# A deformable-convolution network on one core: the offset convolution's last two terms in halves of four rows

## The chip, the cores and the metric

The kernel runs on one core of a Trainium2 chip. The metric is the device time of one execution in microseconds; the kernel before takes 6531.28 us (median of 3 runs, 6528.49 to 6531.62).

A core has five engines that run side by side and wait for each other through semaphores: TensorE (matmuls and transposes, written PE; its weight loads PEld), VectorE (DVE), ScalarE (ACT), GpSimd (POOL) and SyncE (SP). GpSimd and SyncE mostly issue DMAs here. TensorE writes to PSUM only, from which ScalarE or VectorE copy.

## The reference

The input is x of shape 4 x 256 x 64 x 64 in 32-bit floats. A channel normalisation is followed by three modulated deformable 3 x 3 convolutions, then by a mixture of eight experts with two chosen per token. What matters here is one deformable layer:

```python
om = lax.conv_general_dilated(x, w_off, (1, 1), padding=...) + b_off[None, :, None, None]
off = om[:, :2 * K].reshape(B, K, 2, H, W)
mask = jax.nn.sigmoid(om[:, 2 * K:])
ys = gy + base_y + off[:, :, 0]
xs = gx + base_x + off[:, :, 1]
sampled = _bilinear(x, ys, xs) * mask[:, None]
out = jnp.einsum('bikhw,oik->bohw', sampled, w.reshape(O, C, K)) + b
```

K is 9. The first line is the offset convolution: an ordinary 3 x 3 convolution of 256 channels to 27. Its result says for every pixel and tap where to sample, and with what weight.

## The kernel before

An image is worked in 8 blocks of 512 pixels, 8 rows of 64 columns each. With 3 layers and 4 images that makes 96 blocks. Two things are done to each.

**The offset convolution** (`off_block`, L345 and following). It has 18 terms: nine taps (ky, kx), each with two halves c of the channels. A term is one matmul with 128 rows of contraction, 27 (padded to 32) output channels and up to 512 pixels. As 32 outputs use a quarter of TensorE's columns, term m is put into column strip g = m % 4 and adds into its own 32 partitions of the PSUM tile po. Terms with kx = 1 come first and cover all 64 columns of a row (512 pixels); those with kx = 0 or 2 lack one column at the image's edge (8 x 63 = 504 pixels). So strips 0 and 1 get five terms, strips 2 and 3 four. A 32-bit matmul appears as two records in the trace, two passes over the same data, each with a weight load. `om` (L366) takes po out of PSUM on ScalarE with the bias; four matmuls `pm` (L371) add the strips and turn the result, so that pixels lie on partitions; then ScalarE and VectorE work out indices idx and coefficients cf.

**The main block** (`main_block`). For each of 9 taps and 4 groups of 128 pixels, GpSimd gathers the pixels' neighbours from a table in DRAM (`g`, L503, 9 buffers), VectorE interpolates in two operations (L509, L514, the result `s`, 8 buffers), ScalarE scales s by the mask (L517), TensorE transposes (`tp`, L532, 3 PSUM buffers), ScalarE copies to sT (L535), and TensorE multiplies with the layer's weights into acc (L549).

Beside these two, the experts of images that are through are worked in small pieces (ftp L843, ph L859, py L877), the normalisation of the next images is done (tp_pre), and the rows finished are written back as tables.

The program is written as a weave: generators give a few steps each between two taps. From this, a scheduler of the build sets the final order of each engine's instructions by its own estimate of times. Each engine then works in that order, and an instruction that waits holds those behind it. So the matmuls of one offset convolution are often split into runs with other matmuls between.

Of the kernel before, what the change touches and what calls it, by code (L numbers as in the profile page):

```python
# [17 lines left out]
CC = C // P  # L18
# [5 lines left out]
RPB = BLK // W  # L24
# [5 lines left out]
Q = 32  # L30
NQ = P // Q
# [86 lines left out]
class Weave:  # L118
# [226 lines left out]
    def off_block(self, l, b, n, w):  # L345

        nc = self.nc
        nm = f"{l}_{b}_{n}"


        po = self.ps1.tile([P, BLK], F32, tag="po", name=f"po_{nm}")

        terms = [(ky, kx, c) for kx in (1, 0, 2) for ky in range(3) for c in range(CC)]
        for m, (ky, kx, c) in enumerate(terms):
            g = m % NQ
            x0, x1 = max(0, 1 - kx), min(W, W + 1 - kx)
            nc.tensor.matmul(  # L357
                po[g * Q : (g + 1) * Q, :].rearrange("q (r w) -> q r w", w=W)[:, :, x0:x1],
                lhsT=self.wo[l][:, 3 * ky + kx, c, :],
                rhs=w[:, c, ky : ky + RPB, x0 + kx - 1 : x1 + kx - 1],  # L360
                start=(m < NQ),
                stop=(m + NQ >= len(terms)),
                tile_position=(0, g * Q),
            )
        om = self.small.tile([P, BLK], F32, tag="om", name=f"om_{nm}")
        nc.scalar.activation(om, po, AF.Identity, bias=self.bo[l])  # L366
        yield
        pm = self.ps.tile([P, TPB, 3 * K], F32, tag="tp", name=f"pm_{nm}")
        for t in range(TPB):

            nc.tensor.matmul(  # L371
                pm[:, t, :],
                lhsT=om[:, t * P : (t + 1) * P],
                rhs=self.strips[:, : 3 * K],
                start=True,
                stop=True,
            )

        def small(tag, shape=(P, J, 2), dt=F32):
            return self.small.tile(list(shape), dt, tag=tag, name=f"{tag}_{nm}")  # L380

        idx = self.plan.tile([P, J], I32, tag=f"idx{b % 2}", name=f"idx_{nm}")
        cf = self.plan.tile([P, J, 3], F32, tag=f"cf{b % 2}", name=f"cf_{nm}")
        self.plans[l, b, n] = (idx, cf)

        th = small("th", (P, J))
        nc.scalar.activation(
            th.rearrange("p (t k) -> p t k", k=K), pm[:, :, 2 * K :], AF.Tanh, scale=0.5
        )
        pos = small("pos")  # L390
        nc.scalar.copy(pos.rearrange("p (t k) d -> p t (k d)", k=K), pm[:, :, : 2 * K])
        yield
        yield
        with self.after(self.last):
            nc.vector.tensor_tensor(
                pos, pos, self.base[:, n].rearrange("p t k d -> p (t k) d"), ALU.add
            )

        nc.vector.tensor_scalar(pos, pos, -1.0, float(H), ALU.max, ALU.min)
        pi = small("pi", dt=I32)  # L400
        nc.vector.tensor_copy(pi, pos)
        pf = small("pf")
        nc.vector.tensor_copy(pf, pi)
        yield
        up = small("up")
        nc.vector.tensor_tensor(up, pf, pos, ALU.is_gt)
        fl = small("fl")
        nc.vector.tensor_tensor(fl, pf, up, ALU.subtract)

        nfr = small("nfr")  # L410
        nc.vector.tensor_tensor(nfr, fl, pos, ALU.subtract)
        ixf = small("ixf", (P, J))
        nc.vector.scalar_tensor_tensor(
            ixf, fl[:, :, 0], float(TC), fl[:, :, 1], ALU.mult, ALU.add
        )
        nc.vector.tensor_scalar(idx, ixf, float(TC + 1), None, ALU.add)
        yield


        first = small("first")  # L420
        nc.vector.tensor_scalar(first, nfr, 1.0, LEAST, ALU.add, ALU.max)
        inv = small("inv")
        nc.vector.reciprocal(inv, first)
        corner = small("corner", (P, J))
        nc.vector.tensor_tensor(corner, first[:, :, 0], first[:, :, 1], ALU.mult)
        nc.vector.scalar_tensor_tensor(cf[:, :, 0:2], nfr, -1.0, inv, ALU.mult, ALU.mult)
        nc.vector.scalar_tensor_tensor(cf[:, :, 2], th, 1.0, corner, ALU.add, ALU.mult)
# [720 lines left out]
```

## Time and profile before

| | us |
|---|---|
| median of 3 runs | 6531.28 |
| profiled execution | 7434.65 |
| its span, first to last instruction | 7432.9 |
| mean granted TensorE clock, as a share | 0.932 |
| transposes tp (L532), busy | 1227.0 |
| acc (L549), busy | 3442.6 |
| experts ph and py (L859, L877), busy | 683.7 and 658.8 |
| gathers g (L503) on GpSimd, busy | 3650.6 |
| interpolation (L509, L514) on VectorE, busy | 2556.5 and 1656.7 |

The profile is of one execution with the recorder on, which takes longer than a plain run. A group's line gives its busy time, the mean of one instruction in ns, and the idle time of the engine just before it with what ended most of that. A line of waits gives who waited for whom: us in total, number of times, the longest. A line of the timeline gives start and length in us, then engine, line, operation, tiles and shapes, and how many instructions it merges. In the lines of slices each digit is the busy share, or the granted clock, of one fortieth of the span in tenths.

### The profile page before, as it was taken

What the parts mean: (1) busy time and instruction counts of PE and PEld (TensorE: products, weight loads), DVE (VectorE), ACT (ScalarE), POOL (GpSimd) and SP (SyncE); (2) the same over time, 40 slices, a digit from 0 to 9 for tenths busy, and PEclk for the clock granted to TensorE, in tenths of its full rate; (3) what the DMA queues carried; (4) which work ended last, traced back from release to release, by engine and by line L of the source; (5) the groups of instructions that cost most, each with busy time, mean ns of one, the idle gap of its engine ahead of it and who ended that gap; (6) DMA issues with size and microseconds to landing.
All of it is one profiled execution on the core that took longest, in us unless ns stands there. A gap on an engine that the chain in (4) does not pass through costs nothing. (4 is left out here: it accounts for less than half of the span.)

```text
span 7432.9 us, 88104 instructions
## 1 busy us (share of the span) xinstructions
PE 6352.4 (85%) x26500; PEld 3653.7 (49%) x26500; DVE 4932.4 (66%) x11467; ACT 3278.3 (44%) x7139; POOL 4441.2 (60%) x4245
## 2 busy tenths in 40 slices
PE   7888888888888898988877898898887889977887
PEld 3434443444445555555444454454554456644665
DVE  7767776888756666776855676666787554667521
ACT  3444444554444444554443444444453334444322
POOL 4555665666656665555666665665667664666543
PEclk8999999989999999999989999999998899988988
DMA  8889999999879888888888998888998876887644
GB/s 286 312 297 339 346 339 346 362 345 340 321 267 322 311 315 315 310 314 296 282 295 306 327 331 299 318 324 314 325 342 307 281 273 233 286 301 271 229 138 124
DMA packets 805210, 2228.40 MB, mean 300 GB/s; under 512 B 105016, under 2 KB 307768, under 8 KB 798976
## 3 DMA queue, kind: packets, MB, share of 16 engines
q0 software_dynamic: 551200, 1947.35, 73.0%
q1 hardware_dynamic: 253536, 275.41, 11.0%
q8 instruction: 214, 3.51, 0.2%
q14 instruction: 260, 2.13, 0.1%
HBM read 2165.40 MB, written 196.40 MB: 318 GB/s over the span
## 5 line engine op out<-in xcount | busy, mean ns | idle before, releaser
L503 POOL DMA_INDIRECT g<-tab,idx x3456 | 3650.6, 1056 | 2310.7 <-DVE s L514 975.8
L549 PE MATMUL acc<-sT,wk 128*128 128x512 f32 x6912 | 3442.6, 620 | 44.6 <-ACT r L580 17.0
L509 DVE SCALAR_TENSOR_TENSOR g<-g,cf 128x512 f32<-128x512 f32 x3456 | 2556.5, 743 | 274.2 <-DMA g<-tab,idx 249.9
L514 DVE SCALAR_TENSOR_TENSOR s<-g,cf 128x256 f32<-128x256 f32 x3456 | 1656.7, 482 | 1287.5 <-PE tp L532 561.4
L535 ACT COPY sT<-tp 128x512 f32<-128x512 f32 x1728 | 1010.7, 586 | 2052.0 <-PE tp L532 1137.3
L532 PE MATMUL tp<-ident,s 128*128 128x128 f32 x6912 | 1227.0, 287 | 635.7 <-ACT s L517 373.8
L517 ACT ACTIVATE s<-s,cf 128x256 f32<-128x256 f32 x3456 | 1630.8, 508 | 260.7 <-DVE s L514 157.0
L549 PEld LDWEIGHTS acc<-sT,wk 128*128 128x128 f32 x6912 | 1238.3, 200 | 916.2 <-issue 871.5
L532 PEld LDWEIGHTS tp<-ident,s 128*128 128x128 f32 x6912 | 880.9, 147 | 1607.0 <-issue 839.5
L859 PE MATMUL ph<-fzT,w 128*128 128x256 f32 x2608 | 683.7, 401 | 111.1 <-ACT hT L869 74.2
L877 PE MATMUL py<-w,hT 128*128 128x256 f32 x2608 | 658.8, 392 | 39.9 <-ACT hT L869 23.2
L859 PEld LDWEIGHTS ph<-fzT,w 128*128 128x128 f32 x2608 | 498.1, 200 | 256.2 <-ACT hT L869 92.7
L869 ACT ACTIVATE hT<-ph,w 128x256 f32<-128x256 f32 x652 | 279.2, 471 | 695.2 <-PE ph L859 388.3
L877 PEld LDWEIGHTS py<-w,hT 128*128 128x128 f32 x2608 | 486.6, 194 | 180.6 <-issue 69.4
L815 POOL DMA_INDIRECT zt<-z,tok x326 | 330.9, 1015 | 174.2 <-issue 90.3
L803 POOL DMA_INDIRECT w<-in_W,wrow x163 | 175.7, 1078 | 379.3 <-ACT sT L535 134.1
L357 PE MATMUL po<-win,wo 128*32 128x504 f32 (+1 forms) x2304 | 364.1, 613 | 11.2 <-issue 8.3
L918 POOL DMA_INDIRECT gy<-ys,slots x256 | 260.2, 1017 | 106.7 <-issue 79.7
L895 DVE TENSOR_TENSOR y<-py,w 128x512 f32<-128x512 f32 x163 | 111.8, 686 | 316.3 <-PE py L877 242.7
L366 ACT ACTIVATE om<-po,bo 128x512 f32<-128x512 f32 x96 | 66.0, 688 | 365.4 <-PE po L357 228.5
L357 PE MATMUL po<-win_pre,wo 128*32 128x504 f32 (+1 forms) x1152 | 191.2, 628 | 4.1 <-ACT om L366 3.3
L357 PEld LDWEIGHTS po<-win,wo 128*32 128x32 f32 x2304 | 74.4, 111 | 223.8 <-issue 190.5
(154 smaller groups left out, 3029.2 us busy)
## 6 DMA issues: line engine op xcount, KB each, us to landing
tab<-hv SPq DMA_DIRECT2D x512, 128.0 KB
g<-tab,idx POOLq DMA_INDIRECT x3456
ys<-y SPq DMA_DIRECT2D x163, 256.0 KB
tab<-h_pre SPq DMA_DIRECT2D x128, 256.0 KB
wk<-in_conv_w SPq DMA_DIRECT2D x117, 256.0 KB
xc_pre<-in_x SPq DMA_DIRECT2D x32, 512.0 KB
xr_tok<-in_x SPq DMA_DIRECT2D x32, 512.0 KB
t<-t_tok SPq DMA_DIRECT2D x32, 512.0 KB
```

What stands on the lines that cost most here:

```text
L357: nc.tensor.matmul(po[g * Q : (g + 1) * Q, :].rearrange("q (r w) -> q r w", w=W)[:, :, x0:x1], lhsT=self.wo[l][:, 3 * ky + kx, c, :], rhs= ...
L503: self.gathered = nc.gpsimd.indirect_dma_start(out=g.rearrange("p x s f -> p (x s f)"), out_offset=None, in_=self.table(*self.stages[i][:2 ...
L509: nc.vector.scalar_tensor_tensor(g[:, :, 0, :], g[:, :, 1, :], cf[:, j, 0:1], g[:, :, 0, :], ALU.mult, ALU.add,)
L514: self.last = nc.vector.scalar_tensor_tensor(s, g[:, 1, 0, :], cf[:, j, 1:2], g[:, 0, 0, :], ALU.mult, ALU.add)
L517: nc.scalar.activation(s, s, AF.Copy, scale=cf[:, j, 2:3])
L532: self.turned = nc.tensor.transpose(tp[:, c, u * P : (u + 1) * P], ss[u][:, c * P : (c + 1) * P], self.ident)
L535: nc.scalar.copy(self.sT[:, :, t0 * P : (t0 + 2) * P], tp)
L549: nc.tensor.matmul(self.acc[:, o, :], lhsT=self.wk[k][:, c, o * P : (o + 1) * P], rhs=sT[:, c, :], start=(k == 0 and c == 0), stop=(k == K ...
L815: self.nc.gpsimd.indirect_dma_start(out=zt, out_offset=None, in_=grp.zd, in_offset=bass.IndirectOffsetOnAxis(ap=grp.tok[:, j : j + 1], axi ...
L859: nc.tensor.matmul(ph[:, h, :], lhsT=w1[:, o : o + P], rhs=zT[:, c, :], start=(c == 0), stop=(c == CC - 1),)
L869: nc.scalar.activation(ht[:, h, :], ph[:, h, :], AF.Gelu, bias=w1[:, k : k + 1])
L877: nc.tensor.matmul(py[:, u, :], lhsT=hT[h // 2][:, h % 2, u * P : (u + 1) * P], rhs=w2[:, h * C : (h + 1) * C], start=(h == 0), stop=(h == ...
```

## The change

The 18 terms modulo four strips leave two over. These two (kx = 2, ky = 2, both channel halves) are split by rows: each becomes two matmuls over four rows (4 x 63 = 252 pixels), so that 20 matmuls are dealt over the four strips: four full ones and one half in each. The sum of the strips, which pm forms, is the same.

```diff
-        terms = [(ky, kx, c) for kx in (1, 0, 2) for ky in range(3) for c in range(CC)]
-        for m, (ky, kx, c) in enumerate(terms):
+        terms = [
+            (ky, kx, c, 0, RPB) for kx in (1, 0, 2) for ky in range(3) for c in range(CC)
+        ]
+        left = len(terms) % NQ
+        share = RPB * left // NQ
+        terms[-left:] = [
+            (*term[:3], r0, r0 + share)
+            for term in terms[-left:] for r0 in range(0, RPB, share)
+        ]
+        for m, (ky, kx, c, r0, r1) in enumerate(terms):
             g = m % NQ
             x0, x1 = max(0, 1 - kx), min(W, W + 1 - kx)
             nc.tensor.matmul(
-                po[g * Q : (g + 1) * Q, :].rearrange("q (r w) -> q r w", w=W)[:, :, x0:x1],
+                po[g * Q : (g + 1) * Q, :].rearrange("q (r w) -> q r w", w=W)[:, r0:r1, x0:x1],
                 lhsT=self.wo[l][:, 3 * ky + kx, c, :],
-                rhs=w[:, c, ky : ky + RPB, x0 + kx - 1 : x1 + kx - 1],
+                rhs=w[:, c, r0 + ky : r1 + ky, x0 + kx - 1 : x1 + kx - 1],
                 start=(m < NQ),
                 stop=(m + NQ >= len(terms)),
                 tile_position=(0, g * Q),
```

NQ is 4, RPB 8 (rows of a block), so left is 2 and share is 4. The first four matmuls, which start a strip's sum, stay whole.

## The prediction

> **What bounds the kernel now.** I read the page first (busy shares, slices, groups), then the waits engine by engine, then one offset convolution in the timeline.
>
> ```profile
> PE 6352.4 (85%) x26500; PEld 3653.7 (49%) x26500; DVE 4932.4 (66%) x11467; ACT 3278.3 (44%) x7139; POOL 4441.2 (60%) x4245
> PE   7888888888888898988877898898887889977887
> PEclk8999999989999999999989999999998899988988
> DMA  8889999999879888888888998888998876887644
> L357 PE MATMUL po<-win,wo 128*32 128x504 f32 (+1 forms) x2304 | 364.1, 613 | 11.2 <-issue 8.3
> L357 PE MATMUL po<-win_pre,wo 128*32 128x504 f32 (+1 forms) x1152 | 191.2, 628 | 4.1 <-ACT om L366 3.3
> ```
>
> TensorE is at 80 to 90% in every slice, and DMA nearly as high: two resources are close together. The offset convolution (L357) is 555 us of TensorE's 6352, in 3456 records: 96 blocks x 18 matmuls x 2 passes each.
>
> The profiled execution took 7434.65 us, the median run 6531.28; the recording costs 903 us. TensorE's 6352 us of recorded work is 97% of the shorter time, so I expect TensorE to be fuller in a plain run than the page shows. Whether DMA is slowed by the recording the page doesn't say. I count savings as absolute microseconds of TensorE work and take the same number off the median.
>
> ```profile
> PE tp L532 <- ACT s L517: 373.8, 174, 15.9
> POOL g L503 <- DVE s L514: 975.8, 457, 15.4
> DVE s L514 <- PE tp L532: 561.4, 349, 9.7
> DVE g L509 <- DMA g<-tab,idx: 249.9, 98, 10.3
> ACT om L366 <- PE po L357: 228.5, 72, 6.3
> ```
>
> (us in total, times, longest.) Read from the third line: VectorE stands 561 us because transposes haven't freed an s buffer; because VectorE stands, GpSimd waits 976 us for a free gather buffer. That is back pressure from TensorE. Against it stand 250 us in which VectorE waits for a gather's data, which a faster TensorE doesn't shorten. 561 of 811 us, 0.69, is my share of the kernel in which TensorE time is kernel time.
>
> ```profile
> 2027.34 0.16 PEld L357 LDWEIGHTS po<-win,wo 128*32 128x32 f32 x8 [0.76 <-ACT hT L869]
> 2027.34 3.59 PE L357 MATMUL po<-win,wo 128*32 128x512 f32 x28
> 2027.80 0.12 PEld L357 LDWEIGHTS po<-win,wo 128*32 128x32 f32 x4 [0.30 <-issue]
> 2028.23 0.12 PEld L357 LDWEIGHTS po<-win,wo 128*32 128x32 f32 x4 [0.31 <-issue]
> 2028.65 0.12 PEld L357 LDWEIGHTS po<-win,wo 128*32 128x32 f32 x4 [0.31 <-issue]
> 2029.07 0.12 PEld L357 LDWEIGHTS po<-win,wo 128*32 128x32 f32 x4 [0.31 <-issue]
> 2029.49 0.12 PEld L357 LDWEIGHTS po<-win,wo 128*32 128x32 f32 x2 [0.31 <-issue]
> 2029.92 0.12 PEld L357 LDWEIGHTS po<-win,wo 128*32 128x32 f32 x2 [0.31 <-issue]
> 2030.86 0.33 PE L532 MATMUL tp<-ident,s 128*128 128x128 f32 x1
> ```
>
> This is a block's last 14 matmuls, 28 passes. The loads come every 0.42 us in fours, one round ahead of their matmuls: four strips stream together, and a round lasts one stream. The last two loads are x2: terms 16 and 17 sit on strips 0 and 1 only, and two rounds (first and second pass) run with half the array empty. From 2027.34 to 2030.86 are 3.52 us: 8 rounds of 0.424 us plus 0.13 us of emptying the array.
>
> **What the Trainium skill says.** "TensorEngine Tiling (Array Packing)", Key Properties: tiles work independently, and changing the tiling mode drains TensorE. The trace agrees: fours start together, and leaving costs the 0.13 us above. "TensorE: Matmul & The Clock Gate", Part 3: packed matmuls start about 4 ns apart; within a round the records here are some 7 ns apart. The tiling page's Instruction Overhead gives a floor of about 60 cycles for a small free size; 252 columns are far above it. No run shows a 252-column strip matmul yet.
>
> **The change part by part.**
>
> 1. Removed: two rounds of 504 columns per block. Added: two rounds of 252 columns with four strips filled. Each of the four half matmuls has a load and a stream per pass: 2 matmuls, 4 loads and 4 streams more per block. For a round's length there are two bounds. Linear in columns: 0.424 x 252/504 = 0.212 us; the 128-column transposes (four in 0.43 us) against the 512-column acc (four in 1.72 us) support linearity. Load-bound: a strip's load lasts 0.106 to 0.110 us, four of them 7 ns apart, so a round can't be under about 0.13; if the second pass's loads came late I allow 0.30 at most. I take 0.212. Saved: 2 x 0.212 = 0.424 us per block, 96 blocks: 40.7 us. Rounds in stretches of lower clock (mean granted 0.932) are longer and save more. Bounds: at 0.30, 24 us; at 0.212 and the mean clock, 44 us.
>
> 2. Start stagger: the last round has four starts instead of two, 14 ns later for the last one: 96 x 0.014 = 1.3 us lost.
>
> 3. The order. The two kernels' instruction orders, laid side by side, show the same work on every engine apart from these matmuls. GpSimd's queue is unchanged; on SP a single input load (xc_pre_7) moves by four places during start-up, and that costs nothing next to gathers already queued. A block is split into runs, with other matmuls between: before in 252 runs over 96 blocks (42 times as 1, 3, 14 matmuls), after in 246 (39 times as 1, 3, 16; 4, 16 goes from 24 to 32 times). A run of one matmul at 2053.56 lets the next transposes start only at 2054.53: 0.97 us for a single matmul. Joining one costs nothing elsewhere, since a run of four takes the same two rounds. Six runs fewer: about 5 us, put between 0 and 6.
>
> 4. No new wait: the halves read the same window and write the same po, which one om (L366) reads. In front of that om ScalarE stands idle 228 us with the s activations queued behind it, so po's earlier end helps there too; I count it inside part 1.
>
> 5. Moved by the scheduler on ScalarE: about 150 times a copy sT (L535) moves ahead of an s activation (L517), 15 times the reverse. Such a copy waits for its transposes, then takes 0.586 us, and the s behind it waits. Nothing if s was early. TensorE waited for an s before 174 of some 1728 transposes groups, one in ten: 15 of the 150 would hurt, by 0.59 us each, 9 us; bound above by 150 x 0.59 = 88 us. I take nothing in the sum, because the 15 reverse moves and TensorE's earlier end push the other way, and put it in the range.
>
> Sum on TensorE: 40.7 - 1.3 + 5 = 44.4, say 45 us. Times 0.69: 31 us. 7434.65 becomes about 7404 under the recorder, and 6531.28 becomes 6500.
>
> **Rivals.**
>
> - Absorbed: DMA sets the pace (8 or 9 tenths busy; 249.9 us of VectorE waiting for gathers). TensorE then waits longer for s. A conversion of 0.1 to 0.5: 5 to 22 us saved, 6509 to 6526. Against it: the 976 us in which GpSimd can't even issue a gather.
> - More: full conversion plus ScalarE released earlier at om, and rounds at lower clock: 48 to 65 us, 6466 to 6483. For it: TensorE's 97% of the plain time.
> - It doesn't do what it says: halves don't overlap, or a half round costs as much as a full one. Then part 1 is zero and only the run count remains: 6526 to 6533. Against: every four consecutive strip matmuls overlap in the trace, also when a run starts on another strip.
> - Slower: part 5 decides. The sT copies ahead of s delay the transposes, then VectorE and the gathers. It costs 0.59 us plus the wait for the copy's own transposes, say 0.8 us each time it is exposed. It cancels my 31 us from about 40 exposed cases in 150, where the trace suggests 15; at 60 to 100 cases it costs 48 to 80 us, so the time is 6548 to 6580.
>
> **How the numbers follow.** Forecast 0.53 (6490 to 6508), more 0.08, absorbed 0.20, doesn't do what it says 0.05, slower 0.14. A measurement of this kernel tells about 0.2% (13 us) from no change. Faster by more than that: forecast, more, and 0.08 of absorbed, 0.69. Within: the other 0.12 of absorbed and the 0.05: 0.17. Slower 0.14. Range: 6472 to 6540 takes the forecast, the absorbed case, no effect and most of "more"; about 0.17 is left out, nearly all on the slow side. The 24 us bound of part 1 with conversion gives about 6511, inside.
>
> **What would show it.** Each block's last loads come as x4 and x4 instead of x2 and x2, 0.21 us apart, and the run of 16 ends about 3.1 us after its start instead of 3.52. L357's records become 3840, its busy time falls from 555 to about 515 us. If TensorE's busy time falls by 45 us while "tp waits for s" grows by as much, the absorbed case holds. If the wait of tp for s grows by more, with sT waiting in front of s on ScalarE, the slower case holds. Wrong outright: half rounds spaced 0.42 us.

## The result and the profile after

The changed kernel takes 6500.16 us (median of 5 runs, 6491.25 to 6506.63) against 6530.9 us (6528.49 to 6531.62): a ratio of 0.9951, 95% interval 0.9937 to 0.9966, a gain of some 31 us.

The chips of this study fall into two levels. On most, the kernel before takes about 6530 us; on one it takes about 7500 us. The profile that the prediction read, with its span of 7432.9 us and a granted TensorE clock of 0.932, belongs to the upper level, though the times beside it are of the lower one, where the clock is 0.976. A new profile of the unchanged kernel (run a0 below, span 6536.8 us) is therefore the one to hold against the profile after. Three lines of its page, the busy times and the two groups of the offset convolution:

```profile
PE 6070.7 (93%) x26500; PEld 3541.3 (54%) x26500; DVE 4957.5 (76%) x11467; ACT 3335.7 (51%) x7139; POOL 4432.4 (68%) x4245
L357 PE MATMUL po<-win,wo 128*32 128x504 f32 (+1 forms) x2304 | 338.5, 593 | 1.1 <-ACT win L580 0.6
L357 PE MATMUL po<-win_pre,wo 128*32 128x504 f32 (+1 forms) x1152 | 187.0, 618 | 4.1 <-ACT om L366 3.3
```

The same of the changed kernel, whose lines after L352 are numbered eight higher:

```profile
span 6498.1 us, 88881 instructions
PE 6025.0 (93%) x26884; PEld 3542.5 (55%) x26884; DVE 4960.6 (76%) x11467; ACT 3330.6 (51%) x7139; POOL 4424.2 (68%) x4245
L365 PE MATMUL po<-win,wo 128*32 128x504 f32 (+2 forms) x2560 | 306.8, 551 | 1.2 <-ACT win L588 0.6
L365 PE MATMUL po<-win_pre,wo 128*32 128x504 f32 (+2 forms) x1280 | 173.9, 577 | 4.2 <-ACT om L374 3.5
```

The offset convolution has 384 records more and 44.8 us less (525.5 to 480.7). TensorE as a whole loses 45.7 us, so nothing else on it grew. (Such totals move from one execution to the next: a second profile of the changed kernel, run f1 below, has 6037.2 us at a clock of 0.973 where this one has 6025.0 at 0.976. The offset convolution alone agrees to 1.5 us, 480.7 and 479.2.) The span loses 38.7 us between these two executions, and the medians 31 us.

The mechanism is seen in one block's last 16 matmuls in the timeline of the changed kernel (start us, length, then what):

```profile
2089.51 3.17 PE L365 MATMUL po<-win,wo 128*32 128x512 f32 x32
2091.66 0.12 PEld L365 LDWEIGHTS po<-win,wo 128*32 128x32 f32 x4 [0.31 <-issue]
2092.09 0.12 PEld L365 LDWEIGHTS po<-win,wo 128*32 128x32 f32 x4 [0.31 <-issue]
2092.61 0.44 PE L540 MATMUL tp<-ident,s 128*128 128x128 f32 x2
```

The loads now come in fours to the end. They run one round ahead of their matmuls: the load at 2092.09 stands at the start of the first half round and carries the weights of the second. The start times of the last two rounds' matmuls show the half rounds directly. In the profile before they start 0.43 us apart, in that of the changed kernel 0.22 us (granted clock 1.00 in both stretches):

```profile
2029.91 0.59 PE L357 MATMUL po<-win,wo 128*32 128x504 f32 x2
2030.34 0.59 PE L357 MATMUL po<-win,wo 128*32 128x504 f32 x2
```

```profile
2092.08 0.38 PE L365 MATMUL po<-win,wo 128*32 128x252 f32 x4
2092.30 0.38 PE L365 MATMUL po<-win,wo 128*32 128x252 f32 x4
```

From the last load to the next transposes are 0.52 us, two half rounds and the emptying of the array. In the kernel before the same stretch, from 2029.92 to 2030.86, is 0.94 us, two full rounds and the emptying. From the run's start to the next transposes are 3.10 us, where before it was 3.52.

Who waits, in the profile of a0 and then in that of the changed kernel (us in total, times, longest):

```profile
DVE g L509 <- DMA g<-tab,idx: 471.8, 408, 10.3
DVE s L514 <- PE tp L532: 200.0, 197, 5.0
PE tp L532 <- ACT s L517: 202.5, 235, 4.1
ACT om L366 <- PE po L357: 230.5, 88, 5.1
```

```profile
DVE g L517 <- DMA g<-tab,idx: 470.7, 429, 10.9
DVE s L522 <- PE tp L540: 163.2, 163, 4.9
PE tp L540 <- ACT s L525: 200.1, 233, 5.1
ACT om L374 <- PE po L365: 199.0, 88, 4.8
```

VectorE's wait for TensorE falls by 37 us and ScalarE's wait for po by 31 us; the wait for gathers stays. TensorE's wait for s stays as it was (202.5 and 200.1 us), so the scheduler's moves on ScalarE cost nothing that can be seen.

**Where the 31 us came from.** The two executions can be cut at the same copies sT (the 181st, 541st, 1261st and 1601st of 1728). The windows view then shows, for each stretch, its length, the busy time of the engines, the clock, the DMA share and GB/s. First a0, then the changed kernel:

```profile
0.00:665.00 665.00, 599.87 (x2818) 295.82 (x2818) 551.48 (x1458) 342.46 (x758) 401.01 (x413) 0.97 0.96 354
665.00:1791.00 1126.00, 1028.47 (x4355) 537.02 (x4356) 992.72 (x2405) 620.65 (x1311) 771.22 (x728) 0.96 0.99 380
1791.00:4288.00 2497.00, 2408.72 (x10562) 1394.68 (x10561) 1954.45 (x4269) 1339.41 (x2907) 1796.75 (x1699) 0.99 0.96 360
4288.00:5593.00 1305.00, 1224.82 (x5269) 744.09 (x5268) 961.08 (x2120) 672.78 (x1414) 900.88 (x867) 0.99 0.91 334
```

```profile
0.00:664.00 664.00, 592.43 (x2917) 296.58 (x2918) 552.71 (x1459) 343.20 (x758) 400.19 (x413) 0.97 0.96 355
664.00:1785.00 1121.00, 1022.29 (x4434) 536.24 (x4433) 992.11 (x2405) 620.02 (x1311) 774.66 (x728) 0.96 0.99 381
1785.00:4249.00 2464.00, 2382.60 (x10720) 1394.03 (x10719) 1955.48 (x4266) 1335.64 (x2905) 1782.91 (x1699) 0.99 0.97 365
4249.00:5551.00 1302.00, 1217.15 (x5317) 744.50 (x5316) 962.73 (x2121) 671.62 (x1413) 899.99 (x866) 0.99 0.91 335
```

In the first two stretches, with 44 of the 96 blocks, TensorE loses 14 us of work and the time falls by 6. In the third, with 40 blocks, it loses 26 us and the time falls by 33. In the second the DMA engines are busy 0.99 of the time; in the third TensorE is busy 96%. These are single executions, and a stretch is good to some 7 us (run e1 below, with the TensorE work of before, has 2490 us in the third). What the cuts suggested was two regimes, and experiments with the change in parts of the blocks.

### The profile page after: what moved, and what is told of

It is laid out like the page before. It is cut to its first block, busy times and chain, and to the rows that moved or that the text cites. A ratio compares the mean times of both kernels' runs of the same rounds, so it can differ in the third digit from the quotient of the medians.

```text
span 6498.1 us, 88881 instructions
## 1 busy us (share of the span) xinstructions
PE 6025.0 (93%) x26884; PEld 3542.5 (55%) x26884; DVE 4960.6 (76%) x11467; ACT 3330.6 (51%) x7139; POOL 4424.2 (68%) x4245
## 5 line engine op out<-in xcount | busy, mean ns | idle before, releaser
L557 PE MATMUL acc<-sT,wk 128*128 128x512 f32 x6912 | 3317.4, 601 | 13.5 <-ACT win L588 9.2
L525 ACT ACTIVATE s<-s,cf 128x256 f32<-128x256 f32 x3456 | 1669.2, 509 | 688.8 <-DVE s L522 638.2
L557 PEld LDWEIGHTS acc<-sT,wk 128*128 128x128 f32 x6912 | 1193.0, 193 | 833.0 <-issue 800.1
L540 PE MATMUL tp<-ident,s 128*128 128x128 f32 x6912 | 1199.7, 280 | 204.6 <-ACT s L525 200.1
L867 PE MATMUL ph<-fzT,w 128*128 128x256 f32 x2608 | 651.2, 386 | 37.6 <-DMA w<-in_W,wrow 19.4
L867 PEld LDWEIGHTS ph<-fzT,w 128*128 128x128 f32 x2608 | 478.3, 192 | 164.2 <-ACT hT L877 36.4
L365 PE MATMUL po<-win,wo 128*32 128x504 f32 (+2 forms) x2560 | 306.8, 551 | 1.2 <-ACT win L588 0.6
L941 DVE SCALAR_TENSOR_TENSOR ta<-gy,cw,ta 128x256 f32<-128x256 f32 x256 | 120.3, 478 | 100.0 <-DMA gy<-ys,slots 53.5
L365 PE MATMUL po<-win_pre,wo 128*32 128x504 f32 (+2 forms) x1280 | 173.9, 577 | 4.2 <-ACT om L374 3.5
```

What stands on the lines that cost most here:

```text
L365: nc.tensor.matmul(po[g * Q : (g + 1) * Q, :].rearrange("q (r w) -> q r w", w=W)[:, r0:r1, x0:x1], lhsT=self.wo[l][:, 3 * ky + kx, c, :], ...
L525: nc.scalar.activation(s, s, AF.Copy, scale=cf[:, j, 2:3])
L540: self.turned = nc.tensor.transpose(tp[:, c, u * P : (u + 1) * P], ss[u][:, c * P : (c + 1) * P], self.ident)
L557: nc.tensor.matmul(self.acc[:, o, :], lhsT=self.wk[k][:, c, o * P : (o + 1) * P], rhs=sT[:, c, :], start=(k == 0 and c == 0), stop=(k == K ...
L867: nc.tensor.matmul(ph[:, h, :], lhsT=w1[:, o : o + P], rhs=zT[:, c, :], start=(c == 0), stop=(c == CC - 1),)
```

## The experiments

Each run stands beside the kernel before on the same chip. "Theory A" is the prediction's even share of 0.69, "B" a share set by the gathers, "C" that the scheduler's order decides, "A2" that a saving counts in the stretches where TensorE is full and not in the others; A2 was formed after the first four runs.

**a0_before_again**: no edit.

> The kernel before, unchanged, with a new profile. The profile that the prediction was made from had a span of 7432.9 us, while the changed kernel's profile has 6498.1 us, near its plain time. If that first profile was a disturbed execution (and not a cost of recording), this one has a span near 6530 us. Theory A (0.69 of TensorE's time is kernel time): VectorE's waits for tp stay above its waits for gathers. Theory B (the gathers' DMA sets the pace): in a span of 6530 us VectorE waits longer for gathers than for tp, as in the changed kernel (470.7 against 163.2 us).

Ratio 1.0000 (0.9992 to 1.0008), span 6536.8 us. The first profile's extra time is no cost of recording. The waits are those of theory B: 471.8 us for gathers, 200.0 for transposes. TensorE's busy time is 6070.7 us where the first profile had 6352.4. Times the granted clocks, 0.976 and 0.932, both are some 5920 us: the same work at a lower clock (an estimate from these four numbers).

**e1_halves_two_strips**: the 20 matmuls of the change, on two strips.

```diff
-            for term in terms[-left:] for r0 in range(0, RPB, share)
+            for r0 in range(0, RPB, share) for term in terms[-left:]
...
-            g = m % NQ
+            g = m % NQ if m < 16 else (m - 16) % 2
...
-                stop=(m + NQ >= len(terms)),
+                stop=(m >= 14 and m not in (16, 17)),
```

> The same 20 matmuls with halves of four rows, but all four halves on strips 0 and 1, two after each other on each. TensorE's rounds are as long as before, and the instruction order is nearly that of before (27 of 16074 other TensorE instructions moved). Theory A: the gain is the two half-empty rounds alone, so this stands at the time before, 6531 us within 10 us. If splitting itself costs (more loads, more starts), it is slower by up to 0.03 us a block, 3 us. Rival: if halves were cheaper for another reason than the use of four strips, it would be near 6500 us.

6529.57 against 6533.23 us, ratio 0.9995 (0.9987 to 1.0004). The offset convolution takes 524.5 us of TensorE, in a0 525.5. Splitting alone neither costs nor gains; the four strips are what gains.

**e2_one_strip**: the kernel before with both left-over terms on strip 0.

```diff
-            g = m % NQ
+            g = m % NQ if m < 16 else 0
...
-                stop=(m + NQ >= len(terms)),
+                stop=(m >= 13 and m != 16),
```

> The 18 whole terms, the last two both on strip 0: four rounds of 0.42 us with one strip instead of two with two, so TensorE's work grows by 0.85 us a block, 81 us, less 6 runs fewer at 0.98 us, 75 us in sum. Theory A (0.69): 6531 + 52 = 6583 us. Theory B (gathers set the pace, 0.1 to 0.5): 6539 to 6569 us. Theory C (the change's gain came from the order that the scheduler found, not from TensorE's time): no relation, 6510 to 6550 us.

6563.45 us, ratio 1.0049 (1.0036 to 1.0062), 30 us slower. That lies within theory B's range, 20 us under theory A's 6583 and above theory C's range. TensorE's busy time grew by 50 us (6070.7 to 6121.1), that of the offset convolution by 65 (525.5 to 590.1), both less than the 75 us reckoned. The time moved by 0.6 of the first and 0.5 of the second.

**e3_sixteen_terms**: the last two terms left out.

```diff
-        terms = [(ky, kx, c) for kx in (1, 0, 2) for ky in range(3) for c in range(CC)]
+        terms = [(ky, kx, c) for kx in (1, 0, 2) for ky in range(3) for c in range(CC)][:16]
```

> The last two terms of the offset convolution are left out (tap ky = 2, kx = 2, both channel halves); offsets and masks come out a little different. TensorE loses two full rounds a block, 0.85 us, 81 us in sum, and 6 runs, 6 us: 87 us. Theory A (0.69): 6531 - 60 = 6471 us, about twice the gain of the change. Theory B (0.1 to 0.5): 6488 to 6522 us, or no more than the change gave. Theory C (order): no relation, 6490 to 6535 us.

6491.57 us, ratio 0.9935 (0.9921 to 0.9949), 42 us faster. TensorE's busy time fell by 68 us, that of the offset convolution by 86 (525.5 to 439.0): again shares of 0.6 and 0.5. Theory B (6488 to 6522 us) holds and theory A's 6471 us doesn't. The gathers read other places here, but the packets and bytes of their queue are the same. The times follow the offset convolution's time on TensorE in all these runs: +65, -1, 0, -45, -86 us of work against +30, -4, 0, -31, -42 us of time. Theory C, for which there should be no relation, falls, though its range for this run just takes in 6491.57.

**e5_halves_middle, e6_halves_outside, e7_halo_first_whole, e4_halo_row_first**: these four were run together on the chip of the upper level. The first two make the change in parts of the blocks:

```diff
-        left = len(terms) % NQ
+        if (l, b) in {(1, 1), (2, 1), (0, 3), (1, 2), (2, 2)}:
+            left = len(terms) % NQ
...
```

with `not in` for e6. The other two turn the order of the taps' rows, e7 in the kernel before, e4 in the changed one:

```diff
-for kx in (1, 0, 2) for ky in range(3) for c in range(CC)
+for kx in (1, 0, 2) for ky in (2, 1, 0) for c in range(CC)
```

> The change in 40 of the 96 blocks only: those whose offset convolution runs in the middle stretch (about 1790 to 4290 us), where TensorE stands still 88 of 2497 us. Theory A2 (two regimes: TensorE's saving is kernel time where TensorE is full, and lost where the gathers' DMA is): nearly the whole gain of the change, 6500 to 6508 us. Theory A (an even share of 0.69 everywhere): 40 x 0.42 us x 0.69 plus 3 us for runs joined, 14 us, 6517 us. Theory C (order): no relation with the blocks.

> The change in the other 56 blocks only: those of the first 1790 us (DMA busy 0.96 to 0.99) and the last ones. Theory A2: 0 to 8 us gained, 6523 to 6531 us, though TensorE loses 24 us of work here. Theory A: 56 x 0.42 us x 0.69, 16 us, 6515 us. Theory C: no relation.

> The kernel before with the taps in the order ky = 2, 1, 0, so that the first matmul of a block needs the next block's row, as the last ones do. The 18 matmuls then become ready together: 120 runs instead of 249. TensorE saves 1.1 us in each of about 42 blocks that went as 1, 3, 14 and 0.1 us in 24 that went as 4, 14: 48 us, with no half matmuls at all. Theory A and A2: 0.6 to 0.7 of it, 29 to 34 us: 6497 to 6502 us. Theory C (the matmuls that the scheduler had put early filled idle time, and pulling them together costs elsewhere): 6520 to 6550 us.

> The changed kernel with the taps in the order ky = 2, 1, 0: halves and whole runs together, 121 runs, TensorE's work down by about 90 us against before. Theory A and A2: 0.6 to 0.7 of it, 54 to 63 us: 6468 to 6477 us. If the two savings share one idle time: no better than the changed kernel, 6495 to 6505 us.

With the kernel before at 7504.47 us, the ratios were 1.0023 (1.0008 to 1.0038), 1.0023 (1.0012 to 1.0035), 1.0110 (1.0084 to 1.0136) and 1.0076 (1.0052 to 1.0100). None of the expectations in microseconds, made for the lower level, can be judged by them. What they show: on this chip less work in the offset convolution brought nothing, and pulling a block's matmuls together made the kernel slower. The page of e7 has

```profile
span 7593.7 us, 88143 instructions
PE 6364.6 (84%) x26500; PEld 3731.8 (49%) x26500; DVE 4935.4 (65%) x11467; ACT 3282.9 (43%) x7139; POOL 4478.2 (59%) x4245
```

TensorE is at 84% there. VectorE and GpSimd have the same work as in a0 within about 1%. TensorE is busy 294 us longer, at a granted clock of 0.916, and the rest of the 1057 us goes into standing still. In the plain runs the clock falls in the order of the times: 0.927 for the kernel before, 0.925 and 0.924 for e6 and e5, 0.919 for e4, 0.918 for e7 (medians). Whether the lower clock makes the time longer or comes with the longer standing wasn't separated. The changed kernel itself wasn't run at this level, and what it does there stays open.

**f1_after_again**: the changed kernel once more, on chip 1.

> The changed kernel, unchanged, once more against the kernel before, with both on whichever chip this call gets. Two levels of the time before were met: near 6530 us (chip 5) and near 7500 us (chip 10, where the first profile's level also is). If the chip is at 6530 us: the ratio of 0.995 comes back, 6491 to 6510 us. If it is at 7500 us, Theory A2 (TensorE's saving counts only where TensorE is full): TensorE is busy 85% there, and the ratio is 0.998 to 1.002. Theory A (0.69 everywhere): 0.996, 31 us less. Theory C (the order decides): slower, as the four kernels with other orders were on chip 10 (1.002 to 1.011).

6499.46 against 6532.14 us, 0.9952 (0.9939 to 0.9966): the gain comes back. The chip of the first measurement isn't on record, so whether this is a second one is open.

**g1_halves_middle** and **g2_halves_outside**: e5 and e6 at the lower level.

> The change in the 40 blocks of the middle stretch only, a second time, for a chip at 6530 us (if this one is at 7500 us again, it repeats 1.002). Theory A2 (two regimes): nearly the whole gain of the change, 6500 to 6508 us, ratio 0.9955 to 0.9965. Theory A (an even share of TensorE's saving everywhere): 40 of 96 blocks, 14 us, ratio 0.998. Theory C (order): no relation with the blocks.

6514.92 against 6532.28 us, 0.9968 (0.9956 to 0.9980), 21 us by the ratio. That is more than the 14 us of an even share and less than "nearly the whole"; the interval just reaches to both.

> The change in the 56 blocks outside the middle stretch only, a second time. On a chip at 6530 us: the middle blocks alone gave 0.9968 (21 us), so what is left of the change's 0.9952 is some 10 us. Theory A2: a ratio of 0.998 to 1.000 for more than half of the blocks. Theory A (an even share): 56 of 96 blocks, 18 us, ratio 0.9972.

6527.05 against 6530.54 us, 0.9994 (0.9985 to 1.0003): some 4 us from 56 blocks, at most 10, where an even share gives 18 us and lies outside the interval. The saving was made: the offset convolution takes 26 us less of TensorE than in a0 (499.8 against 525.5), in g1 21 us less (504.2). In g2's profile TensorE as a whole loses only 11 us, at a clock of 0.974 against 0.976. So 42% of the blocks carry two thirds of the change's gain, and the other 58% little. In the windows view g1 and g2, cut at the same copies as above, have the third stretch at

```profile
1791.00:4259.00 2468.00, 2384.89 (x10707) 1392.07 (x10706) 1956.58 (x4269) 1339.35 (x2906) 1790.66 (x1699) 0.99 0.97 364
```

```profile
1788.00:4280.00 2492.00, 2405.23 (x10577) 1395.18 (x10578) 1955.51 (x4268) 1339.11 (x2905) 1795.87 (x1700) 0.99 0.97 361
```

against 2497 us in a0 and 2464 in the changed kernel. g1 has the shorter stretch, g2 hardly: the time falls where the halves are, if TensorE is full there.

**g3_halo_row_first**: e4 at the lower level.

> The changed kernel with the taps in the order ky = 2, 1, 0 (121 runs instead of 243), a second time. On a chip at 6530 us: TensorE's work falls by about 90 us against before; at the 0.6 to 0.7 that one strip (+50 us of work, +30 us) and sixteen terms (-68 us, -42 us) showed, 54 to 63 us: ratio 0.9903 to 0.9917, which beats the changed kernel. Theory C (the early matmuls had filled idle time, pulling them together costs elsewhere, as at 7500 us where it gave 1.0076): 0.996 or more.

6486.51 against 6532.17 us, 0.9929 (0.9914 to 0.9945), some 46 us. That falls short of the range expected, whose edge the interval touches, and lies outside theory C's 0.996 or more. It is faster than the kernel before by more than the changed kernel is (0.9951 and 0.9952), but the intervals overlap. TensorE's busy time fell by 97 us (6070.7 to 5974.0), of which less than half is time. In the third stretch (2468 us long) TensorE now stands still for 101 us, in a0 for 88: with less to do, it begins to wait there too. On the one chip of the upper level the same kernel was slower, so the gain is shown for the lower level only.

**All traces of the lower level, cut in the same way.** For each kernel, from the windows view of the tile po and of the whole: by how many us the offset convolution's time on TensorE differs from a0 in the first two stretches together and in the third, how long these stretches are, and the change of the whole time by its ratio.

| kernel | stretches 1, 2: work | length | stretch 3: work | length | whole time |
|---|---|---|---|---|---|
| a0, before | 0 | 1791 | 0 | 2497 | 0 |
| e1, two strips | +1 | 1786 | -2 | 2490 | -3 |
| changed | -16 | 1785 | -23 | 2464 | -32 |
| f1, changed again | -18 | 1790 | -22 | 2463 | -31 |
| g1, halves in 40 blocks | -1 | 1791 | -20 | 2468 | -21 |
| g2, halves in 56 blocks | -15 | 1788 | -5 | 2492 | -4 |
| e2, one strip | +25 | 1791 | +29 | 2512 | +32 |
| e3, sixteen terms | -32 | 1788 | -45 | 2447 | -42 |
| g3, changed, rows turned | -56 | 1765 | -48 | 2468 | -46 |

From 25 us more work to 32 us less, the first two stretches keep their length within 6 us; the third gets longer and shorter with its own work. The change of the whole time is close to the work added or taken in the third stretch alone, within 9 us in every row. That is theory A2, seen in kernels that weren't made to test it. Only g3 departs from it in part: its first two stretches are shorter by 26 us and its third gives back 29 of 48. With 56 us less work, TensorE's time seems to count in the first two as well, or the other order of matmuls does; the runs don't part the two.

## Why the prediction was right, and where its reasons were not

- **The half rounds.** 0.212 us each, linear in the columns: right. A run of 16 ends 3.10 us after its start, as forecast. The sign given for it, last loads 0.21 us apart, was wrong, since loads come one round ahead of their matmuls; they stand 0.42 us apart, which read alone would look like the sign of being wrong. The matmuls are what starts 0.21 us apart.
- **Start stagger.** Taken as 7 ns for each further matmul of a round, 1.3 us in all. That spacing holds for the first round of a run (2027.342 to 2027.362). In the last rounds the first and the last start are 7 ns apart both before, with two matmuls (2030.337 and 2030.344), and after, with four (2092.296 and 2092.303). The term is nothing.
- **TensorE's sum.** Forecast 44.4 us, measured 45.7, and 44.8 in the offset convolution alone. e1 shows that splitting without the two added strips gains nothing, so the concurrency is the cause.
- **Fewer runs.** The traces have 249 runs before and 243 after, six fewer, as the orders said (252 and 246 there). g3 beside the changed kernel, with the same matmuls in 121 runs, has 73 us less in the offset convolution (407.5 against 480.7), 0.6 us for each run that is gone. Six would be some 4 us, an estimate that fills what the half rounds' 40.7 leave of 44.8. In the time it isn't shown by itself.
- **ScalarE's moved copies.** Taken as nothing, and the wait of transposes for s is 202.5 and 200.1 us: right. The slower rival falls with it, for chips of the lower level. ScalarE's wait for po fell by 31 us, a help that the prediction named.
- **The share of 0.69.** This step gave the right number for a wrong reason, by luck. The measured share is 31 of 45.7 us, 0.68, but 0.5 to 0.6 in e2 and e3 and 0.5 in g3, so it isn't a constant of this kernel. It was taken as 561 us of waits for transposes against 250 us for gathers from a profile of the upper level. In the profile of a0 the same sum is 200.0 and 471.8 us, a share of 0.30, which would have forecast a gain of 13 us and a time near 6517. The ratio of these two waits isn't a measure of it. What comes close is the chain of waits of a0:

```profile
PE 64%; DMA 12%; DVE 10%; issue 5%; POOL 4%; ACT 4%; SPq 0%; DVEq 0%; POOLq 0%; ACTq 0%
PE acc L549 31%; DMA g<-tab,idx 10%; PE tp L532 9%; PE ph L859 7%; PE py L877 6%; PE po L357 6%; DVE g L509 4%; DVE s L514 3%; POOL g L503 2%; ACT s L517 1%; PE pm L371 1%; POOL gy L918 1%; PE lp_tok L621 1%; POOL zt L815 1%; PE tpv L325 1%
```

The chain of work that ended last goes through TensorE for 64% of the span and through po for 6%, some 392 us of its 525.5: about three quarters of that work lie on it. Its agreement with the measured share is one case, not a proof.

- **An even share.** The prediction spread the saving over all blocks. g1, g2 and the table show otherwise: the absorbed rival holds for most of the 56 blocks, and in the third stretch the saving passes on at about its full size. In the changed kernel 33 us of time came from 26 us of TensorE work there. Some 7 us are within the spread of single executions (e1's 2490 us); ScalarE's earlier release at om may have a part, which wasn't separated.
- **"The recording costs 903 us".** Wrong, as is the sentence that a recorded execution takes longer: the profiled executions of a0 and of the changed kernel take as long as their plain runs. So the 6352 us of TensorE work, "97% of the shorter time", were those of a lower clock; a0 has 6071, 93%. The page also had seven slices at 7 tenths, so "80 to 90% in every slice" was misread.

## What to carry to other kernels

Hold the span of a profile and its granted clock against the plain runs before reading anything from it: 14% more was not the recorder here but another level of the chip, with other waits and a clock of 0.932 instead of 0.976. Work taken off an engine became time only in the stretch where that engine was full; cut the profile into stretches and count the saving in each, and if in doubt make the change in a part of the blocks. Judge a saving by the group of instructions that was changed, as the engine's total moved by 12 us between two executions of one kernel. With column strips, left-over terms were worth splitting over the free dimension, as a round lasted as long as its longest strip.

## What the runs showed of the hardware that was not expected

Streams in column strips scale down: a round of strip matmuls of 252 columns in 32-bit floats takes half of a 504-column round (0.21 us against 0.42), four at a time, with the loads hidden.

And the same kernel takes 6530 us on four chips (1, 3, 5 and 12) and 7504 us on one (10), at granted clocks of 0.976 and 0.927. Between the first profile and a0, both of the kernel before, TensorE's busy time differs as the clocks do, and the gathers' queue is a little longer. Its share of the 16 DMA engines, of a0 and of the first profile:

```profile
q0 software_dynamic: 551200, 1947.35, 79.3%
```

```profile
q0 software_dynamic: 551200, 1947.35, 73.0%
```

79.3% of 6536.8 us are 5184 us, 73.0% of 7432.9 us are 5426 us: the same packets took 5% longer, the kernel 14%. Where the rest comes from stays open.
